# Query projection of 16 of 32 head groups by seven products of quarters, with the squares of the keys summed on ScalarE, in a gated two-layer decoder on one core

## The chip, the cores and the metric

The kernel runs on one core of a Trainium2 chip, written in Bass with the Tile framework, in float32 throughout. The metric is the device time of one execution in microseconds (us), the median of several executions. Inside a core five engines work side by side, each through its own list of instructions in order: TensorE (PE in the profile, with its weight loads as PEld) multiplies matrices into PSUM, VectorE (DVE), ScalarE (ACT) and GpSimd (POOL) work on elements, and SyncE (SP) issues transfers (DMA). ACT and POOL issue some transfers too, and then they are held in their own list until the issue is done.

## The reference, cut to what matters

x has 4 x 512 rows of 512 columns. A first layer (an attention over 256-column context rows and a linear layer of bit weights) is added to x with gates. Then comes the part that fills most of the time, cross attention with 16 heads of 128 columns, and last a layer of 16 experts for the first 512 rows, each row going to up to four of them:

```python
q = (layernorm(x) @ Wq).reshape(B, Sq, H, D)      # 512 -> 16 x 128
k = (ctx @ Wk).reshape(B, Skv, H, D)              # 256 -> 16 x 128
v = (ctx @ Wv).reshape(B, Skv, H, D)
q = q * rsqrt(mean(q*q, -1) + EPS) * gq           # rmsnorm of each head
k = k * rsqrt(mean(k*k, -1) + EPS) * gk
attn = softmax(einsum('bqhd,bkhd->bhqk', q, k) / sqrt(D))
x = x + tanh(g_xattn[1]) * (einsum('bhqk,bkhd->bqhd', attn, v).reshape(...) @ Wo)
x = x + tanh(g_ffn[1]) * experts(layernorm(x))    # only the first batch's rows are read and changed
```

## The kernel before

**Groups and steps.** The 16 heads are taken two at a time: a group m is one batch and one pair of heads, so there are 32 groups, eight for each of four batches, and 64 heads. After the first layer the program runs 64 steps, one for each head: step i is head h = i % 2 of group m = i // 2. A step has four quarters. Each quarter begins with `scores`, one matmul of 128 query rows against all 512 keys of this head, and then runs pieces of other work that a table assigns to it. An even step (h = 0) makes the keys and values of the next group (`keys_values`, quarters 0 and 1), the values product of an earlier head (`values(i - 2)`, quarter 2) and half of an output projection (`project`, quarter 3). An odd step (h = 1) makes the two heads' queries of the next group (`queries`, quarters 0 and 1), `values(i - 2)` in quarter 2 and the other half projection in quarter 3.

**The expert blocks.** From step 22 to step 55 each pair of steps also carries one expert block: rows turned (`rows_T`, even step, quarter 0), the two hidden products (`hidden`, quarters 1 and 2) with Tanh and product on ACT and DVE (`gate`, `gated`), then in the odd step the turned hidden rows (`hidden_T`, quarter 0) and `down` in quarter 2, whose result `keep_rows` stores. The rows are gathered back and added to x near the end (`add_row`).

**Order.** The order on every engine is the order in which the Python program emits instructions; nothing reorders it. `tick()` counts emitted matmuls, and `later(n, f)` emits f when n more have been counted. So work for DVE, ACT and POOL is put behind the matmul it belongs to by counts, and a list that waits holds up all that stands behind it.

**A score's way.** `scores` writes one of two PSUM banks (psS). On DVE the rows are scaled and their minimum taken in one instruction (L870, which empties the bank), ACT takes the exponential with its sum (L871), DVE takes the reciprocal (L877), scales (L878) and transposes in blocks of 32 into tP (L260). After a head's fourth such transpose SP issues 16 transfers of 64 KB (L268), which bring tP into the form that `values` reads (pT, tag big).

**Keys.** `keys_values` copies each PSUM bank into kn and v on ACT. Two ticks after its last matmul ACT squares all of kn in one instruction (L748); at four ticks DVE sums the squares (L752) and forms kss (L755), POOL raises to the power -1/2 (rk, L192) and multiplies kn by it (L759); at eleven ticks DVE transposes kn in blocks into tK (L770). ACT then issues one store to DRAM (k_d) and, at 18 ticks, four loads of kT.

**Queries.** `queries(m, h)` makes one head's queries, transposed, with 128x128 blocks of Wq as weights and 512 columns of the normalised, transposed rows (lx1, tag lnT) as the moving operand. ACT reads the bank twice, once for squares and once to scale into qT. The squares are then summed by DVE, PE and POOL into rq, which L870 uses for scaling.

```python
for k in range(KC):                                    # KC = 4
    nc.tensor.matmul(pp, wq[:, k, h * D : (h + 1) * D], lx1[b][:, k, :], ...)
```

The tag psA has three PSUM banks, which keys, queries, hidden, down and half of the projections take in turn; psO has one and psT two. wq, wkv and wo have two SBUF buffers each and are loaded by SP. In the profile a matmul of the code has two records.

Of the kernel before, what the change touches and what calls it, by code (L numbers as in the profile page):

```python
# [31 lines left out]
FCH = [(0, 128), (128, 128), (256, 96)]  # L32
NSLOT = 2 * NE - 1
SPILL = 1
TB = 32
# [19 lines left out]
def tile_gated_decoder(  # L55
# [51 lines left out]

    def col(n, tag):
        return tiny.tile([P, n], F32, tag=tag, name=tag)

# [95 lines left out]
    def rows_stats(b):  # L206

        stats = {}

        def chunk(c):  # L210
            if c == 0:
                stats["mv"] = tiny.tile([P, NC, 2], F32, tag="mv", name="mv")
            st = col(6, "st")
            nc.vector.bn_stats(st, x_sb[:, b * NC + c, :])
            nc.vector.bn_aggr(stats["mv"][:, c, :], st)
            if c == NC - 1:
                ve = col(NC, "ve")
                nc.vector.tensor_scalar(ve, stats["mv"][:, :, 1], EPS, None, ALU.add)
                stats["rs"] = col(NC, "rs")
                rsqrt(stats["rs"], ve, NC)  # L220

        return [lambda c=c: chunk(c) for c in range(NC)], stats

    def normalised(b, c, mv, rs):
        xn = row("xn", 2)
        nc.vector.tensor_scalar(
            xn, x_sb[:, b * NC + c, :], mv[:, c, 0:1], rs[:, c : c + 1], ALU.subtract, ALU.mult
        )
        return xn
# [96 lines left out]
    def l0_stats(b):  # L326

        pieces, stats = rows_stats(b)

        def gates():  # L330
            gate0[b] = gr = col(NC, "gr")
            nc.vector.tensor_scalar(gr, stats["rs"], tg[:, 0:1], None, ALU.mult)
            gm = col(NC, "gm")
            nc.vector.scalar_tensor_tensor(gm, stats["mv"][:, :, 0], -1.0, gr, ALU.mult, ALU.mult)
            for c in range(NC):
                x_c = x_sb[:, b * NC + c, :]
                later(c, lambda x_c=x_c, c=c: nc.scalar.activation(
                    x_c, x_c, AF.Identity, bias=gm[:, c : c + 1]
                ))

        return pieces[:-1] + [lambda: (pieces[-1](), later(3, gates))]
# [75 lines left out]
    def layer0_attention():  # L417
# [57 lines left out]

        load_wq(0)
        load_wq(1)
        load_wo(0)
# [15 lines left out]
        for h in range(G):  # L494
            queries(0, h)
        linear(NB - 1, turned0[NB - 1], [0, 1])

# [19 lines left out]
    def route():  # L517
# [20 lines left out]

        zero = row("xg", 1)
        nc.gpsimd.memset(zero, 0.0)  # L540
# [10 lines left out]
        ef_b = ef.unsqueeze(1).broadcast_to(CE)  # L551
        hit = small_tile([P, TOPK, NC, NE], "hit")
        for k in range(TOPK):
# [103 lines left out]
    def bias_row():  # L657
# [23 lines left out]
        yield  # L681
        brow.append(row("y", 2))
        nc.vector.tensor_copy(brow[0], pb)
# [17 lines left out]
    wq_of, wo_of = {}, {}  # L701
    q_of, sq_of, rq_of, kn_of, k_of, v_of, o_of = {}, {}, {}, {}, {}, {}, {}
    turned, moved, ends = {}, {}, {}
    n_heads = G * len(groups)

    def load_wq(m):
        t = work.tile([P, KC, GD], F32, tag="wq", name="wq")
        nc.sync.dma_start(t, wq_v[:, :, cols(m)])
        wq_of[m] = t

# [6 lines left out]
    def keys_values(m, chunks):  # L717
# [28 lines left out]
        def squares():  # L746
            st["sq"] = work.tile([P, NC, GD], F32, tag="sq", bufs=1, name="ksq")
            nc.scalar.activation(st["sq"], kn, AF.Square)  # L748

        def scale():  # L750
            kss = col(NC * G, "kss")
            nc.vector.tensor_reduce(  # L752
                kss, st["sq"].rearrange("p c (h d) -> p (c h) d", h=G), AX.X, ALU.add
            )
            nc.vector.tensor_scalar(kss, kss, 1.0 / D, EPS, ALU.mult, ALU.add)  # L755
            rk = col(NC * G, "rk")
            rsqrt(rk, kss, NC * G)
            kn_v = kn.rearrange("p c (h d) -> p c h d", h=G)
            nc.gpsimd.tensor_tensor(  # L759
                kn_v, kn_v,  # L760
                rk.rearrange("p (c h) -> p c h", h=G).unsqueeze(3).broadcast_to([P, NC, G, D]),
                ALU.mult,
            )
# [27 lines left out]
        later(2, squares)  # L791
        later(4, scale)
        later(11, turn)
# [3 lines left out]
    def queries(m, h):  # L797
# [21 lines left out]
        if h < G - 1:  # L819
            return  # L820
        n = G * S // TB
        st = {}

        def part():

            st["part"] = col(n, "part")
            nc.vector.tensor_reduce(
                st["part"], sq.rearrange("p h (j r) -> p (h j) r", r=TB), AX.X, ALU.add,
                apply_transpose=True,
            )  # L830
# [6 lines left out]
        def scale():  # L837

            own = col(n, "own")
            nc.vector.tensor_tensor(own, st["pq"][:, 0:n], mine, ALU.mult)  # L840
            v = col(G * NC, "qss")
            nc.vector.tensor_reduce(v, own.rearrange("p (c a) -> p c a", a=NT), AX.X, ALU.add)
            nc.vector.tensor_scalar(v, v, 1.0 / D, EPS, ALU.mult, ALU.add)  # L843
            rq_of[m] = col(G * NC, "rq")
            rsqrt(rq_of[m], v, G * NC)
# [319 lines left out]
    for c in range(NC):  # L1165
        for k in range(TOPK):
            put(last + 1 + c, k, lambda c=c, k=k: add_row(c, k))
    for b in range(1, NB):
        i = (b - 1) * NG * G + NG
        for j, f in enumerate(turned_rows(b, lx1, lnt)):  # L1170
            put(i + j // NC * (1 + j % NC), 3 if j >= NC else j, f)
        if b > 1:
            put(i, 3, lambda b=b: load_ctx(b))
# [13 lines left out]
    def step(i):  # L1187
        m, h = divmod(i, G)
        pieces = [[], [], [], []]
        if i >= G:  # L1190
            pieces[0 if i == n - 1 else 2].append(lambda: values(i - G))
        elif h > 0:
            pieces[3].append(lambda: tick(8))
        if i == n - 1:
# [7 lines left out]
        if h == 0:  # L1202
            if 0 < m < M - 1:
                pieces[0].append(lambda: keys_values(m + 1, [0, 1]))
                pieces[1].append(lambda: keys_values(m + 1, [2, 3]))
            if m + 2 < M:
                pieces[1].append(lambda: load_wq(m + 2))
                pieces[3].append(lambda: load_wkv(m + 2))
            if m >= 2:
                pieces[3].append(lambda: project(m - 2, [2, 3]))  # L1210
            if 2 <= m < M:
                pieces[3].append(lambda: later(4, lambda: load_wo(m)))
        elif i < n - 1:
            if m + 1 < M:
                pieces[0].append(lambda: queries(m + 1, 0))
                pieces[1].append(lambda: queries(m + 1, 1))
            if m >= 1:
                pieces[3].append(lambda: project(m - 1, [0, 1] if m < M else [0, 1, 2, 3]))
        for quarter in range(4):
            if i < n:  # L1220
                scores(i, quarter)
            for f in pieces[quarter] + extra.get((i, quarter), []):
                f()
# [73 lines left out]
```

## Time and profile before

| what | value |
|---|---|
| runs | 1455.59, 1457.45, 1457.69 us; median 1457.45 |
| profiled execution | 1457.03 us, span of the profile 1454.8 us |
| mean granted TensorE clock | 0.995 |
| busy in the span: PE, DVE, ACT, POOL | 1425.9, 936.0, 523.2, 285.5 us |
| matmuls of the queries (L807) | 512 records of 128x512, 231.3 us busy |
| matmuls of the scores (L856), keys and values (L733) | 512 records each, 262.5 and 231.8 us busy |
| squares of the keys (L748, ACT), their sums (L752, DVE) | 32 each, 1059 and 1216 ns in the mean |
| transfers of probabilities (L268) | 1008 of 64 KB, 2.0 us from issue to landing |

The lines of the profile name the line of the code, the engine, what is written and what is read, the shape and the count; behind the bar stand busy time, the mean length of one, and the engine's idle time before it with what ended it. The mean length of one matmul is longer than its share of the array, since matmuls run one behind the other in a pipeline: the interval between two starts is what a matmul costs.

### The profile page before, as it was taken

The page shows a single profiled execution, that of the slowest core. Times are in us where ns is not written, and L with a number is a line of the kernel's source. Part 1 is how long each engine was busy: PE and PEld are TensorE (multiplying, and loading weights), DVE is VectorE, ACT ScalarE, POOL GpSimd, SP SyncE. Part 2 cuts the span into 40 slices and gives each one's busy share as a digit, 9 for nine tenths or more (in the row PEclk, how much of TensorE's full clock was granted, in tenths as well). Part 3 has the DMA queues.
Part 4 walks back from the last instruction along what each step waited for, and adds up shares of the span by engine and source line. Part 5 has one row for each costly group of instructions (what it writes and reads, how often), then busy time and mean ns, then how long its engine had stood idle before and what let it go on. Part 6 is the DMA issues. An engine that isn't in the chain of part 4 may idle for free.

```text
span 1454.8 us, 13743 instructions
## 1 busy us (share of the span) xinstructions
PE 1425.9 (98%) x3745; PEld 669.9 (46%) x3745; DVE 936.0 (64%) x2160; ACT 523.2 (36%) x1196; POOL 285.5 (20%) x210
## 2 busy tenths in 40 slices
PE   7999998999999999999999999999999999999998
PEld 3544443444444444444444444444444444444444
DVE  4768857677776776665655565565565565557783
ACT  4642223333443334233333323333333323333331
POOL 1314414332111111111110111111011111002320
PEclk9999999999999999999999999999999999999999
DMA  7525016644544445555565565557566566635752
GB/s 254 174 73 189 1 44 162 158 131 132 136 133 136 134 134 171 170 173 177 174 173 175 174 215 168 170 165 200 158 185 191 144 200 192 177 113 162 200 145 77
DMA packets 155347, 226.90 MB, mean 156 GB/s; under 512 B 24576, under 2 KB 90640, under 8 KB 155264
## 3 DMA queue, kind: packets, MB, share of 16 engines
q1 hardware_dynamic: 127312, 177.86, 41.6%
q10 hardware_dynamic: 23040, 33.56, 7.4%
q0 software_dynamic: 4912, 14.53, 3.6%
q8 instruction: 33, 0.54, 0.2%
q14 instruction: 50, 0.41, 0.1%
HBM read 129.62 MB, written 30.17 MB: 110 GB/s over the span
## 4 chain that ended last, share of the span: by engine, by line
PE 81%; DVE 9%; ACT 3%; DMA 3%; SPq 3%; issue 1%; POOL 0%; ACTq 0%; POOLq 0%
PE psA L733 14%; PE psS L856 13%; PE psA L807 12%; PE psO L903 12%; PE psA L954 7%; PE psA L1029 6%; PE psO L954 4%; PE psT L954 3%; PE psA L1057 3%; PE psA L363 3%; SPq L268 3%; PE psA L691 1%; DMA big<-tP 1%; ACT prob L871 1%; DVE prob L870 1%; DVE tP L260 1%
## 5 line engine op out<-in xcount | busy, mean ns | idle before, releaser
L871 ACT ACTIVATE prob<-prob,top 128x512 f32<-128x512 f32 x256 | 184.8, 722 | 571.9 <-DVE prob L870 571.9
L856 PE MATMUL psS<-kT,qT 128*128 128x512 f32 x512 | 262.5, 596 | 1.0 <-DVE prob L870 1.0
L733 PE MATMUL psA<-wkv,ctx 128*128 128x512 f32 x512 | 231.8, 592 | 0.3 <-ACT v L728 0.3
L807 PE MATMUL psA<-lnT,wq 128*128 128x512 f32 x512 | 231.3, 592 | 0.0
L903 PE MATMUL psO<-big,v 128*128 128x512 f32 x504 | 226.6, 592 | 0.0
L870 DVE TENSOR_SCALAR_CACHE_REDUCE prob<-psS,rq 128x512 f32<-128x512 f32 x256 | 187.7, 734 | 53.2 <-PE psS L856 47.6
L260 DVE STREAM_TRANSPOSE tP<-prob 128x512 f32<-128x512 f32 x252 | 179.1, 711 | 9.0 <-DVE prob L878 1.1
L877 DVE RECIPROCAL rden<-den 128x1 f32<-128x1 f32 x256 | 40.7, 159 | 215.1 <-ACT prob L871 214.8
L807 PEld LDWEIGHTS psA<-lnT,wq 128*128 128x128 f32 x512 | 96.7, 190 | 118.6 <-issue 118.4
L903 PEld LDWEIGHTS psO<-big,v 128*128 128x128 f32 x504 | 95.7, 190 | 120.7 <-issue 116.2
L733 PEld LDWEIGHTS psA<-wkv,ctx 128*128 128x128 f32 x512 | 96.5, 190 | 118.8 <-issue 112.6
L192 POOL TENSOR_TENSOR rq<-qss,mhalf 128x8 f32<-128x8 f32 x32 | 53.2, 1661 | 493.0 <-DVE qss L843 493.0
L878 DVE TENSOR_SCALAR prob<-prob,rden 128x512 f32<-128x512 f32 x256 | 137.3, 536 | 9.0
L192 POOL TENSOR_TENSOR rk<-kss,mhalf 128x8 f32<-128x8 f32 x32 | 52.6, 1645 | 439.0 <-DVE rden L877 277.8
L856 PEld LDWEIGHTS psS<-kT,qT 128*128 128x128 f32 x512 | 92.9, 190 | 89.3 <-issue 68.9
L954 PE MATMUL psA<-wo,oT 128*128 128x512 f32 x256 | 123.3, 601 | 5.8 <-ACT oT L910 5.8
L1029 PE MATMUL psA<-gu,xgT 128*128 128x352 f32 x272 | 86.0, 459 | 0.0
L954 PEld LDWEIGHTS psA<-wo,oT 128*128 128x128 f32 x256 | 48.3, 191 | 68.3 <-issue 57.6
L770 DVE STREAM_TRANSPOSE tK<-kn 128x256 f32<-128x256 f32 x128 | 45.4, 412 | 39.1 <-POOL kn L759 39.1
L1029 PEld LDWEIGHTS psA<-gu,xgT 128*128 128x128 f32 x272 | 51.7, 190 | 37.9 <-issue 16.3
L954 PE MATMUL psO<-wo,oT 128*128 128x512 f32 x128 | 62.8, 613 | 0.0
L275 DVE SCALAR_TENSOR_TENSOR x_sb<-psA,tg,x_sb 128x512 f32<-128x512 f32 x80 | 57.8, 723 | 6.7 <-PE psA L691 3.8
(173 smaller groups left out, 1483.4 us busy)
## 6 DMA issues: line engine op xcount, KB each, us to landing
big<-tP SPq DMA_DIRECT2D x1008, 64.0 KB, 2.0
k_d<-tK ACTq DMA_DIRECT2D x32, 512.0 KB, 2.6
kT<-k_d ACTq DMA_DIRECT2D x128, 128.0 KB, 2.9
wq<-in_wq_dram SPq DMA_DIRECT2D x32, 512.0 KB, 3.7
wo<-in_wo_dram SPq DMA_DIRECT2D x32, 512.0 KB, 4.4
gu<-in_gate_dram SPq DMA_DIRECT2D x16, 704.0 KB
gu<-in_up_dram SPq DMA_DIRECT2D x16, 704.0 KB, 6.3
wkv<-in_wk_dram SPq DMA_DIRECT2D x32, 256.0 KB, 5.6
```

The costliest lines, as they stand in the source:

```text
L192: nc.gpsimd.tensor_tensor(out, v, mhalf[:, :n], ALU.pow)
L260: nc.vector.transpose(tP[:, :, c, :], e.rearrange("p (j r) -> p j r", r=TB))
L275: nc.vector.scalar_tensor_tensor(x_sb[:, t, :], src, gate, x_sb[:, t, :], ALU.mult, ALU.add)
L733: nc.tensor.matmul(pp, ctxs[b][:, k, c * P : (c + 1) * P], wkv[:, k, :, :].rearrange("p a n -> p (a n)"), start=(k == 0), stop=(k == CC - 1),)
L807: nc.tensor.matmul(pp, wq[:, k, h * D : (h + 1) * D], lx1[b][:, k, :], start=(k == 0), stop=(k == KC - 1))
L856: nc.tensor.matmul(sc, q_of[m][h][:, c * P : (c + 1) * P], k_of[m][:, :, h, :], start=True, stop=True)
L870: nc.vector.tensor_scalar(e, x, scale, 3.0e38, ALU.mult, ALU.min, accum_out=top)
L871: nc.scalar.activation(st["e"], st["e"], AF.Exp, bias=top, scale=-1.0, accum_out=st["den"])
L878: nc.vector.tensor_scalar(st["e"], st["e"], rden, None, ALU.mult)
L903: nc.tensor.matmul(po, v[:, k, h * D : (h + 1) * D], pT[:, :, k, :], start=(k == 0), stop=(k == NC - 1))
L954: nc.tensor.matmul(pp, oT[:, j, c * P : (c + 1) * P], wo[:, j, :], start=(j == 0), stop=(j == G - 1))
L1029: nc.tensor.matmul(st[a][:, :FF], st["xgT"][:, k * P : (k + 1) * P], st["gu"][:, a, k, :], start=(k == 0), stop=(k == KC - 1),)
```

## The change

The change has four parts.

1. **Seven products.** For the groups q with 12 <= q < 28 the queries of both heads are made together. Weights (two halves of the depth, two heads) and rows (two halves of the depth, two halves of the rows) are quarters of a 2x2 product, which seven products of quarters give instead of eight. The sums of weights are made by POOL (`combine`, four of 128x256 for each group), the sums of rows by DVE once for each batch (`combine_rows`, four of 128x512, for three batches). Each product is two matmuls of 256 columns. Four products are made in quarter 3 of the even step (`quarter_queries(q, 0)`), three in quarter 1 of the odd step (`quarter_queries(q, 1)`), in two banks (px, py) that are held in between; DVE (five additions of 128x256) and ACT (two copies) put the four results together. ACT then squares and scales both heads from SBUF.
2. **Order in these steps.** `values` in the odd step moves from quarter 2 to quarter 0; `project` of a group stands in quarters 2 and 3 of one odd step, behind `down`, instead of in an odd and the next even step; the loads of wo and wkv move with it.
3. **Keys' squares.** In all 32 groups ACT squares kn in eight instructions of 128x128, each with its sum (`accum_out`), two at a tick from the second to the fifth; DVE's sum is gone, and `scale` stands at six ticks instead of four.
4. **Buffers and places.** wq has one buffer instead of two, so its load waits for the last product with the old weights (group 1's is issued behind group 0's queries). Some tiles share tags (xn with y, a zero tile with xgT, brow with xg, hit with tK), and small columns have fewer buffers. The sixteen `add_row` stand three to a step over six steps instead of four to a step over four.

```diff
+SWITCH = (12, 28)
...
     def normalised(b, c, mv, rs):
-        xn = row("xn", 2)
+        xn = row("y", 2)
...
-        load_wq(0)
-        load_wq(1)
+        load_wq(0)()
...
         for h in range(G):
             queries(0, h)
+        load_wq(1)()
...
+    HS, HK = S // 2, KC // 2
+
     def load_wq(m):
-        t = work.tile([P, KC, GD], F32, tag="wq", name="wq")
-        nc.sync.dma_start(t, wq_v[:, :, cols(m)])
-        wq_of[m] = t
+        w = work.tile([P, KC, GD], F32, tag="wq", bufs=1, name="wq")
+        nc.sync.dma_start(w, wq_v[:, :, cols(m)])
+        if not by_quarters(m):
+            wq_of[m] = w
+            return lambda: None
+        sums = work.tile([P, 3, HK, D], F32, tag="wqs", bufs=1, name="wqs")
+        def quarter(h, a):
+            return w[:, a * HK : (a + 1) * HK, h * D : (h + 1) * D]
+        def combine():
+            s1, s2, s4 = (sums[:, j] for j in range(3))
+            s3 = quarter(1, 0)
+            nc.gpsimd.tensor_tensor(s1, quarter(1, 0), quarter(1, 1), ALU.add)
+            nc.gpsimd.tensor_tensor(s2, s1, quarter(0, 0), ALU.subtract)
+            nc.gpsimd.tensor_tensor(s3, quarter(0, 0), s3, ALU.subtract)
+            nc.gpsimd.tensor_tensor(s4, quarter(0, 1), s2, ALU.subtract)
+            wq_of[m] = [quarter(0, 0), quarter(0, 1), s4, quarter(1, 1), s1, s2, s3]
+        return combine
+
+    def combine_rows(b):
+        t = lx1[b]
+        sums = work.tile([P, 4, HK, HS], F32, tag="lxs", bufs=1, name="lxs")
+        def quarter(a, c):
+            return t[:, a * HK : (a + 1) * HK, c * HS : (c + 1) * HS]
+        t1, t2, t3, t4 = (sums[:, j] for j in range(4))
+        nc.vector.tensor_tensor(t3, quarter(1, 1), quarter(0, 1), ALU.subtract)
+        nc.vector.tensor_tensor(t1, quarter(0, 1), quarter(0, 0), ALU.subtract)
+        nc.vector.tensor_tensor(t2, quarter(1, 1), t1, ALU.subtract)
+        nc.vector.tensor_tensor(t4, quarter(1, 0), t2, ALU.subtract)
+        lxs_of[b] = [quarter(0, 0), quarter(1, 0), quarter(1, 1), t4, t1, t2, t3]
...
         def squares():
-            st["sq"] = work.tile([P, NC, GD], F32, tag="sq", bufs=1, name="ksq")
-            nc.scalar.activation(st["sq"], kn, AF.Square)
+            st["kss"] = col(NC * G, "kss", 3)
+            sq = work.tile([P, NC, GD], F32, tag="sq", bufs=1, name="ksq")
+            def chunk(c):
+                for h in range(G):
+                    at = slice(h * D, (h + 1) * D)
+                    nc.scalar.activation(
+                        sq[:, c, at], kn[:, c, at], AF.Square,
+                        accum_out=st["kss"][:, c * G + h : c * G + h + 1],
+                    )
+            for c in range(NC):
+                later(c, lambda c=c: chunk(c))
         def scale():
-            kss = col(NC * G, "kss")
-            nc.vector.tensor_reduce(
-                kss, st["sq"].rearrange("p c (h d) -> p (c h) d", h=G), AX.X, ALU.add
-            )
+            kss = st["kss"]
...
-        later(4, scale)
+        later(6, scale)
...
+    def quarter_queries(m, part):
+        ws, xs = wq_of[m], lxs_of[groups[m][0]]
+        def product(j, out, start):
+            for k in range(HK):
+                nc.tensor.matmul(
+                    out, ws[j][:, k, :], xs[j][:, k, :], start=start and k == 0, stop=k == HK - 1,
+                    skip_group_check=True,
+                )
+                tick(0.5)
+        if part == 0:
...
+            def second():
+                nc.scalar.copy(u2, px[:, 0:HS])
+                nc.vector.tensor_tensor(u2, px[:, HS:S], u2, ALU.add)
+            def fourth():
+                nc.vector.tensor_tensor(u3, py[:, 0:HS], u2, ALU.add)
+                nc.vector.tensor_tensor(q1[:, HS:S], py[:, HS:S], u3, ALU.add)
+            product(0, px[:, 0:HS], True)
+            product(5, px[:, HS:S], False)
+            later(0, second)
+            product(6, py[:, 0:HS], True)
+            product(4, py[:, HS:S], False)
+            later(0, fourth)
+            return
...
+        def upper():
+            nc.scalar.copy(q0[:, 0:HS], px[:, 0:HS])
+            nc.vector.tensor_tensor(q1[:, 0:HS], px[:, HS:S], u3, ALU.add)
+        def lower():
+            nc.vector.tensor_tensor(q0[:, HS:S], py[:, HS:S], u2, ALU.add)
+            for h in (1, 0):
+                nc.scalar.activation(sq[:, h, :], q_of[m][h], AF.Square)
+            for h in (0, 1):
+                nc.scalar.activation(q_of[m][h], q_of[m][h], AF.Identity, scale=gqk)
+        product(1, px[:, 0:HS], False)
+        product(3, px[:, HS:S], True)
+        later(0, upper)
+        product(2, py[:, HS:S], False)
+        later(0, lower)
+        square_sums(m, sq)
...
-            put(last + 1 + c, k, lambda c=c, k=k: add_row(c, k))
+            put(last + 1 + (c * TOPK + k) // 3, (c * TOPK + k) % 3, lambda c=c, k=k: add_row(c, k))
...
+        if (b + 1) * NG > SWITCH[0]:
+            put(2 * max(b * NG, SWITCH[0]) - 2, 1, lambda b=b: combine_rows(b))
...
+        q = m + 1
+        late, late_before = by_quarters(q), by_quarters(m)
         if i >= G:
-            pieces[0 if i == n - 1 else 2].append(lambda: values(i - G))
+            pieces[0 if i == n - 1 or h and late else 2].append(lambda: values(i - G))
...
+            if late and q < M:
+                pieces[3].append(lambda: quarter_queries(q, 0))
         elif i < n - 1:
-            if m + 1 < M:
-                pieces[0].append(lambda: queries(m + 1, 0))
-                pieces[1].append(lambda: queries(m + 1, 1))
+            if q < M and not late:
+                pieces[0].append(lambda: queries(q, 0))
+            if q < M:
+                pieces[1].append(lambda: (quarter_queries if late else queries)(q, 1))
+            if m + 2 < M:
+                pieces[2].append(lambda: later(6, load_wq(m + 2)))
+            if late:
+                pieces[2].append(lambda: project(m - 1, [0, 1]))
             if m >= 1:
-                pieces[3].append(lambda: project(m - 1, [0, 1] if m < M else [0, 1, 2, 3]))
+                pieces[3].append(lambda: project(m - 1, [2, 3] if late else [0, 1]))
+            if late and q < M:
+                pieces[3].append(lambda: later(2, lambda: load_wo(q)))
```

## The prediction

> **What bounds the kernel now.** I read the page's totals first, then busy time by stretch (its length, then busy PE, PEld, DVE, ACT and POOL with their instructions, clock, DMA share, GB/s), then PE's own waits.
>
> ```profile
> PE 1425.9 (98%) x3745; PEld 669.9 (46%) x3745; DVE 936.0 (64%) x2160; ACT 523.2 (36%) x1196; POOL 285.5 (20%) x210
> ...
> 440.00:480.00 40.00, 40.00 (x96) 17.77 (x95) 27.27 (x62) 16.22 (x37) 5.17 (x3) 1.00 0.50 143
> ...
> 880.00:920.00 40.00, 40.00 (x107) 19.07 (x106) 23.38 (x54) 13.28 (x31) 6.24 (x4) 1.00 0.59 179
> ...
> PE psA L954 <- ACT oT L910: 5.8, 5, 2.9
> ...
> PE psS L856 <- DVE prob L870: 1.0, 1, 1.0
> ```
>
> From 280 to 1360 us PE is busy in practically all of every 40 us, DVE in 22 to 31, ACT in 12 to 17. A busy PE can hide short gaps, so I counted: between 560 and 1240 us stand 1364 matmuls of 512 columns, 256 of 352, 141 of 128 and 32 of 32, and at the intervals found below they fill 679 of the 680 us. So TensorE is the bound, and its time saved in the expert stretch is time saved, as long as nothing else becomes late. The second line of waits shows how little is late today.
>
> **The cost of a narrow matmul.** The timeline of PE has unbroken rows of three widths (start, length, count). "us" runs from the first start to the last end, so the interval is (length less the mean duration of one) over (count less one).
>
> ```profile
> 894.06 3.60 PE L807 MATMUL psA<-lnT,wq 128*128 128x512 f32 x8
> ...
> 922.52 2.53 PE L1029 MATMUL psA<-gu,xgT 128*128 128x352 f32 x8
> ...
> 1443.93 1.05 PE L934 MATMUL psA<-big,v 128*128 128x128 f32 x8
> ```
>
> 512 columns: (3.60 - 0.592)/7 = 0.430 us. 352: (2.53 - 0.459)/7 = 0.296. 128: (1.05 - 0.275)/7 = 0.111. The line through the outer two gives 0.297 at 352, as measured, and 0.217 at 256. Each of these has a weight load of its own, recorded with 190 ns, and even at 111 ns between matmuls it does not show. A matmul of the code is two records (float32 goes in two passes: 32 groups of 8 in the code, 512 in the group's count). So the queries of one group cost 16 x 0.430 = 6.88 us; by quarters 7 products x 2 x 2 = 28 records x 0.217 = 6.08. Saved: 0.80 us a group, and for the 16 groups 12 to 27 **12.8 us**. The bounds are half of a wide one (0.215: 13.8 us) and the next wider row (0.296: a loss of 22.5 us); the line through both neighbours says the first is near.
>
> A rule speaks against this. The Trainium skill, "TensorE: Matmul & The Clock Gate", section "Back-to-back issue gap", gives about 81 ns a matmul at N=128 and 131 ns at N=512 for streams with weight loads: a narrow one would keep 62% of a wide one's price. By that, 256 columns would cost about 75% of 512, an estimate from that page, and the change would lose some 34 us. The rows here have 26%, in this kernel's own type, so they decide.
>
> **ScalarE's squares, in the expert steps.** One square of 128x1024 (1.07 us) and a DVE reduction (1.21) become eight of 128x128 with a sum each. The trace has no such form. Between: 0.25 us (a 128-column copy lets the next start 0.16 later, and reading a sum adds 0.09 behind L871) and 0.45 (266 ns for such a copy plus 188 for reading the sum, nothing overlapped). I take 0.33, nearer the overlap that every ACT row shows. ACT grows by 8 x 0.33 - 1.07 = 1.6 us a group and by about 0.9 in the quarter groups (two more copies and squares from SBUF), against 23 idle us in 40: no bound. What matters is who waits behind it. After the change four of the eight stand ahead of gate's Tanh (room: 923.25 to 925.09) and four behind the third softmax exponential.
>
> ```profile
> 923.25 1.07 ACT L748 ACTIVATE ksq<-kn 128x1024 f32<-128x1024 f32 x1
> ...
> 925.09 0.46 ACT L1038 ACTIVATE hh<-psA 128x352 f32<-128x352 f32 x1 [0.77 <-PE psA L1029]
> ...
> 926.81 0.72 ACT L871 ACTIVATE prob<-prob,top 128x512 f32<-128x512 f32 x1 [1.26 <-DVE prob L870]
> ...
> 897.55 2.40 ACTq L785 DMA_DIRECT2D kT<-k_d  x2
> 900.00 0.37 ACT L1050 COPY hT<-psT 128x256 f32<-128x256 f32 x1 [3.18 <-DMA kT<-k_d]
> ...
> 906.40 2.74 PE L1057 MATMUL psA<-dn,hT 128*128 128x512 f32 x6
> ```
>
> That exponential ends at 927.61, so the key factors kss come at 927.61 + 4 x 0.33 = 928.9 where L755 stood at 927.94: 1.0 us later (0.7 to 1.5). Behind kss on DVE wait the key transposes and the fourth softmax; behind that one's last step the sixteen DMAs of the probabilities; and behind some of those ACT waits, because the four loads of kT that it issues wait for them (the row of 2.40 us). The new add into u (about 0.40, from the 0.48 of L1043's 352 columns) also stands ahead of that transpose. So ACT comes free about 1.45 us later (1.1 to 1.9), and its next work is hT, which the block's last matmul, down, needs. Down itself moves forward: from the end of hidden_T (897.98) it was 8.42 us away; now there lie a score, the three last products (12 records) and a score: 0.86 + 12 x 0.217 + 0.86 less 0.16 of drain = 4.15. The copies begin 2.0 to 2.2 us after hidden_T in ten of the seventeen blocks and 2.5 to 3.1 (mean 2.83) in seven. Then 1.45 later, 0.47 to a copy done and seen: the ten just fit (4.0), the seven miss by 0.6. **Cost: 4 us**, 2 at the low end, 10 at the high. Nothing of this waits today.
>
> **The other edits of these steps.** DVE gets five additions of 128x256 a group (2.0 us) for the reduction of 1.21, and has 16 idle us of 40. Its stretch from down to the next step becomes dense: I place the next step's first softmax about 2.5 us later than now, and it catches up in the 3.2 us that DVE idles ahead of gate (922.36 to 925.58). Cost 0; if not, the fourth key matmul waits for its bank, under 1 us a group. Values moves ahead in odd steps, to the first quarter: its probabilities land about 12.6 us into the step before, 15 with that lag, and it lasts 22. Project goes behind down with all four chunks, so oT's copy gets 7 us instead of 0.9: a small gain. The weights' four sums on POOL, 128x256, are 0.6 to 0.8 us each by L688 (1306 ns at 512 columns): 3 us a group on an engine that is idle four fifths, queued behind rq, so no softmax waits for them; the load they wait for (3.7 us to land) is issued past the probabilities' DMAs on SP and has over 20 us until its first product. combine_rows, four additions of about 0.6, falls three times into DVE's idle time. The single wq buffer makes load_wq wait for the group's last product; SP has y_d's store and the next probabilities behind it, and both come later anyway. All 0.
>
> **The squares elsewhere.** The 16 plain groups have a lock in their path. In ten of them DVE's scaling of the fourth probabilities (0.49 us) meets POOL's product on kn and ends 0.28 us after it, whenever that ends:
>
> ```profile
> 376.76 1.90 POOL L759 TENSOR_TENSOR kn<-kn,rk 128x1024 f32<-128x1024 f32 x1
> ...
> 377.28 1.66 DVE L878 TENSOR_SCALAR prob<-prob,rden 128x512 f32<-128x512 f32 x1
> ```
>
> After the change both hang on kss: POOL's product starts 0.26 + 1.72 = 1.98 us after it, the scaling about 1.88. If the scaling goes first, the probabilities leave about 1.3 us earlier, ACT's wait ends earlier and part of the 5.8 us of PE's waits for oT goes, and with it the half clock behind the two long ones (0.91 and 0.92 in the 10 us behind 1360; some 1.7 us each). With squares at 0.45 the order is the same, 0.9 later. I take **-1.5 us**, from -6 (all waits gone) to +4 (a new wait of 0.3 in most).
>
> The Trainium skill, "SBUF — State Buffer", section "Who interferes with whom", has this as an exclusive lock and adds DVE operations with two SBUF inputs; it would make POOL's 3 us of new sums block DVE. The rows above agree on the lock; on two inputs no run here decides. If all of it fell on the path it would be 3 us a group, 48 in all, an estimate by that page; I count none, since DVE has idle time behind it.
>
> **The rest.** Tags shared in layer 0 and the later load of wq for group 1 (issued about 193 us, needed at 208.75) cost 0. Three output additions a step instead of four take DVE work of 0.72 us out of steps with PE waits (2.1 us at 1366) and put it beside the 1.0 at 1410: 0, within 2 either way.
>
> **Sum.** -12.8 + 4 - 1.5 = -10.3. The profiled execution took 1457.03 (span 1454.8 and 2.2 around it), so 1446.7; the median of the runs is 0.4 above it: **1447.0**.
>
> **The rivals.** (a) My forecast: faster, own range 1441.5 to 1454, chance 0.75. (b) ACT becomes the late engine: in every quarter group down waits for hT, or project for ACT's copies of the halves. Price: the shift beyond 1.6 us times 16; it decides from 0.8 us a group, where 12.8 is eaten; at 1.0 the time is 1457.5 + 3.2 = 1460.7. For it: the margin falls from 5.9 us to 0.15, and ACT waits for DMAs there in every block. Against: squares would have to take over 0.45 us. Chance 0.11, slower. (c) The plain groups lose what the others gain: squares at 0.45 and the lock unchanged make 0.9 us later, of which some 0.5 in 15 groups reaches PE, 7 us, with 4 in the others: 1456, no change to speak of; chance 0.10. (d) Narrow matmuls gain nothing: at 0.246 us for 256 columns 28 equal 16 wide ones; with the 4 us of waits 1461. Three rows on one line speak against it: slower, 0.04.
>
> Measurement tells 0.2%, about 3 us, from no change. Faster 0.78 (a, and 0.03 of c), same 0.07 (the rest of c), slower 0.15 (b and d). The range runs from (a)'s low end to part of (b), **1441.5 to 1458**.
>
> **What would show it.** PE: 448 records of 256 columns, 217 ns apart (eight in about 1.9 us); the counts of the old form halved; busy share unchanged. ACT: squares 0.33 apart. PE's waits: down on hT's copy, some 0.6 us in seven blocks, and fewer for oT. Scaling of the fourth probabilities at 0.49 us in the plain groups. I am wrong if down waits in all blocks, if PE shows idle time at the first or last product, or if a product's interval is over 0.23.

## The result, and the profile after

The changed kernel takes 1445.16 us in the median of six runs (before, in the same comparison: 1456.56); the ratio is 0.9917, with an interval of 0.9901 to 0.9934. One of the six, at a mean clock of 0.753, is left out of that ratio; the other five lie between 1441.6 and 1447.56, with a median of 1444.19. The forecast was 1447.0, range 1441.5 to 1458, faster. The profiled execution took 1444.19 (span 1442.5) against 1457.03 (1454.8): 12.8 us less, of which 12.3 in the span.

The totals of the page after. PE has 192 records more and 17 busy us less; ACT has gained 51.6 us, POOL 46.9, DVE 3.1.

```profile
PE 1408.8 (98%) x3937; PEld 703.2 (49%) x3937; DVE 939.1 (65%) x2220; ACT 574.8 (40%) x1708; POOL 332.4 (23%) x274
```

Busy time by stretch (length, then PE, PEld, DVE, ACT and POOL with their instructions, clock, DMA share, GB/s). As before, PE is busy throughout in plain and in expert stretches, so TensorE is still the bound.

```profile
440.00:480.00 40.00, 40.00 (x96) 17.89 (x95) 27.06 (x60) 17.01 (x58) 8.70 (x5) 1.00 0.44 131
880.00:920.00 40.00, 40.00 (x120) 21.70 (x119) 24.04 (x58) 16.30 (x51) 9.09 (x8) 1.00 0.60 181
```

The timeline of PE in an expert block of after: the first of the three last products and, behind the other two and a score, `down`.

```profile
769.09 1.03 PE L880 MATMUL psA<-lnT,wq 128*128 128x256 f32 x4
...
772.54 1.88 PE L1168 MATMUL psA<-dn,hT 128*128 128x512 f32 x4
```

Four narrow matmuls take 1.03 us and one alone 0.379 in the mean, so the interval is (1.03 - 0.379)/3 = 0.217 us, as the prediction has it; their weight loads (190 ns) do not show. hidden_T starts once in each block. In after (first fence) two such starts are 41.82 us apart, in before (second) 42.64:

```profile
851.53 0.49 PE L1159 MATMUL psT<-ident,hh 128*128 128x128 f32 x3
893.35 0.49 PE L1159 MATMUL psT<-ident,hh 128*128 128x128 f32 x3
```

```profile
854.85 0.49 PE L1048 MATMUL psT<-ident,hh 128*128 128x128 f32 x3
897.49 0.49 PE L1048 MATMUL psT<-ident,hh 128*128 128x128 f32 x3
```

That is 0.82 us a group where nothing waits, 13 us in sixteen groups. What waits is in PE's own waits of after (us in total, times, longest):

```profile
PE psT L245 <- DVE y L227: 4.6, 7, 1.1
...
PE psS L967 <- DVE x_sb L276: 2.8, 1, 2.8
...
PE psA L1065 <- issue: 2.0, 1, 2.0
PE psA L1168 <- ACT hT L1161: 1.9, 2, 0.9
PE psS L967 <- DMA kT<-k_d: 1.3, 1, 1.3
```

The wait for oT that led before (5.8 us, five times) is down to 1.1, and the 2.0 of the row with "issue", which is the same matmul at 248 us. Two waits are new in the expert steps: the transposes of the normalised rows (L245; four of the seven waits, 3.6 us between starts; the others are in layer 0), and `down` (L1168). I also summed the gaps between PE's starts beyond the intervals of their widths, and the summed gaps are what "gaps" means below. Between 560 and 1285 us they were 3.4 us before and are 9.2 after: 5.8 us are given back there. Elsewhere they fall by 4.0 us: 2.9 near 85 us, where before has half a clock for 6.8 us; 1.5 between 200 and 560 us; 4.0 between steps 56 and 60, where a wait of 2.1 us and the half clock behind it are gone; and a new wait of 2.84 us at 1397 takes 4.65 back with its own half clock. So PE's last matmul ends 11.2 us earlier (-12.8 + 5.8 - 4.0, to 0.2), and what follows it is 1.1 us shorter.

### The profile page after: what moved, and what is told of

It is laid out like the page before. It is cut to its first block, busy times and chain, and to the rows that moved or that the text cites. A ratio compares the mean times of both kernels' runs of the same rounds, so it can differ in the third digit from the quotient of the medians.

```text
span 1442.5 us, 14876 instructions
## 1 busy us (share of the span) xinstructions
PE 1408.8 (98%) x3937; PEld 703.2 (49%) x3937; DVE 939.1 (65%) x2220; ACT 574.8 (40%) x1708; POOL 332.4 (23%) x274
## 4 chain that ended last, share of the span: by engine, by line
PE 75%; DVE 12%; ACT 5%; DMA 3%; issue 2%; POOL 2%; SPq 1%; ACTq 0%; POOLq 0%
PE psA L775 13%; PE psS L967 12%; PE psO L1014 12%; PE psA L1065 6%; PE psA L857 6%; PE psA L880 5%; PE psA L1140 5%; PE psO L1065 3%; PE psT L1065 3%; PE psA L1168 2%; PE psA L364 2%; DVE x_sb L276 2%; ACT prob L982 2%; PE psA L694 1%; DVE prob L981 1%
## 5 line engine op out<-in xcount | busy, mean ns | idle before, releaser
L967 PE MATMUL psS<-kT,qT 128*128 128x512 f32 x512 | 262.4, 596 | 4.1 <-DVE x_sb L276 2.8
L775 PE MATMUL psA<-wkv,ctx 128*128 128x512 f32 x512 | 231.7, 592 | 0.3 <-ACT v L770 0.3
L981 DVE TENSOR_SCALAR_CACHE_REDUCE prob<-psS,rq 128x512 f32<-128x512 f32 x256 | 187.9, 736 | 27.9 <-PE psS L967 18.7
L775 PEld LDWEIGHTS psA<-wkv,ctx 128*128 128x128 f32 x512 | 96.5, 190 | 118.8 <-issue 108.6
L989 DVE TENSOR_SCALAR prob<-prob,rden 128x512 f32<-128x512 f32 x256 | 140.8, 550 | 9.0
L967 PEld LDWEIGHTS psS<-kT,qT 128*128 128x128 f32 x512 | 92.9, 190 | 78.7 <-issue 60.7
L857 PE MATMUL psA<-lnT,wq 128*128 128x512 f32 x256 | 115.6, 592 | 0.0
L857 PEld LDWEIGHTS psA<-lnT,wq 128*128 128x128 f32 x256 | 48.3, 190 | 59.3 <-issue 59.1
L795 ACT ACTIVATE ksq<-kn 128x128 f32<-128x128 f32 x256 | 75.3, 299 | 0.0
L276 DVE SCALAR_TENSOR_TENSOR x_sb<-psA,tg,x_sb 128x512 f32<-128x512 f32 x80 | 58.2, 727 | 6.7 <-PE psA L694 3.8
```

The source lines that it names most:

```text
L276: nc.vector.scalar_tensor_tensor(x_sb[:, t, :], src, gate, x_sb[:, t, :], ALU.mult, ALU.add)
L775: nc.tensor.matmul(pp, ctxs[b][:, k, c * P : (c + 1) * P], wkv[:, k, :, :].rearrange("p a n -> p (a n)"), start=(k == 0), stop=(k == CC - 1),)
L967: nc.tensor.matmul(sc, q_of[m][h][:, c * P : (c + 1) * P], k_of[m][:, :, h, :], start=True, stop=True)
L981: nc.vector.tensor_scalar(e, x, scale, 3.0e38, ALU.mult, ALU.min, accum_out=top)
L989: nc.vector.tensor_scalar(st["e"], st["e"], rden, None, ALU.mult)
```

## The experiments

My theory from the two traces: the products earn some 13 us, waits in the expert steps take 5.8 back, and the rest comes from the squares and from the clock. The main rival: the squares and the placing of steps gave the gain, and the products earned nothing after their waits.

**1. No quarters at all.**

```diff
-SWITCH = (12, 28)
+SWITCH = (32, 32)
```

> All 32 groups make their queries by eight wide products (SWITCH = (32, 32)); squares, tags, single wq buffer and the placing of the added rows stay as changed. Theory (the products earn 16 x 0.80 = 12.8 us and the new waits of the expert steps take 5.8 of them back: 2.2 for the turned hidden rows, 3.6 for the normalised rows): 1445.2 + 7.0 = 1452, within 2. Rival (the gain is the squares' and the placing's, and the seven products earn nothing after their waits): 1445. Second rival (the waits belong to the squares, not to the products, and stay): 1445.2 + 12.8 = 1458.

Measured: 1450.3 us, ratio 0.9961 (0.9948 to 0.9974). So the products are worth 6.1 us against after's median of 1444.19, and 6.4 by the ratios, where 7.0 were expected; the two intervals do not touch. The sum of gaps between 560 and 1285 us is 4.0 here: the waits of the expert steps came with the products, or with the order of these steps, which this edit takes back too. The profiled execution (span 1446.0) is one of this kernel's better ones: it has no half clock while PE works and only 2.1 us of gaps behind 1360 us, where after has 6.1.

**2. One square again, in the changed kernel.**

```diff
-                    nc.scalar.activation(sq[:, c, at], kn[:, c, at], AF.Square, accum_out=...)
+            nc.scalar.activation(st["sq"], kn, AF.Square)
...
+            nc.vector.tensor_reduce(kss, st["sq"].rearrange(...), AX.X, ALU.add)
-        later(6, scale)
+        later(4, scale)
```

> The changed kernel with the keys' squares as before: one square of 128x1024 on ScalarE, summed by VectorE, scaled at four ticks. Theory (steps 0 to 22, which hold plain groups alone, came out 2.2 us shorter, and in the quarter groups the sums cost the two waits for the turned hidden rows of 2.2): both vanish, 1445, within 2. Rival (VectorE's lag in the quarter groups is what counts, and the reduction of 1.21 us a group makes it worse): 1448 to 1452. Second rival (ScalarE's longer list is what costs, as the forecast had it): 1441.

Measured: 1447.84, ratio 0.9946 (0.9927 to 0.9965); the interval touches that of after. The waits say more: oT is late again, 7.3 us in four waits, 4.1 of them at 252 us.

```profile
PE psA L1057 <- ACT oT L1013: 7.3, 4, 4.1
```

So the sums on ScalarE shorten the way of the probabilities. `down` waits once, by 0.5 us, where after has 1.1 twice, so the wait for hT comes for the most part from the new squares, as the theory has it. The transposes of the normalised rows still wait (3.9 us with layer 0; in the expert steps 2.6, in two places, for 3.6 in four), so most of that wait does not come from the squares.

**3. The sums on ScalarE, alone, in the kernel before.** The edit is that of 2 the other way round.

> The kernel before with the eight squares and their sums on ScalarE alone, scaled at six ticks. Theory (in the plain groups the new form is worth about -0.2 us a group, as steps 0 to 22 show, and in the expert steps nothing waits): 1456.6 - 2 to -4 = 1453.5. Rival (c) of the prediction (later scaling reaches TensorE in the plain groups): 1458 to 1463. No effect: 1456.6.

Measured: 1450.71, ratio 0.9966 (0.9954 to 0.9978): 5.7 us less: more than the 2 to 4 of the theory, and the other way than rival (c). The wait for oT at 252 us falls from 3.08 us to 0.87, the one of 2.28 at 1368 is gone, and so are the two half clocks behind them (1.7 us each); a wait of 1.98 for transfers at 254 is new. In PE's waits oT is left with:

```profile
PE psA L962 <- ACT oT L918: 1.1, 2, 0.7
```

Runs 2 and 3 complete a square with before and after. By the ratios, the products with their order and the old squares (run 2) stand 7.9 us below before, the new squares alone (run 3) 5.0, and both together 12.1: the two gains nearly add up.

**4. Added rows by four, as before.**

```diff
-            put(last + 1 + (c * TOPK + k) // 3, (c * TOPK + k) % 3, lambda c=c, k=k: add_row(c, k))
+            put(last + 1 + c, k, lambda c=c, k=k: add_row(c, k))
```

> The changed kernel with the sixteen added rows four to a step over four steps, as before. Theory (the new wait of 2.84 us at 1397 and the half clock behind it, 4.65 us from step 60 to step 63, come from the added rows that now stand there; the 4.0 us gained in steps 56 to 60 come from their leaving): the two change places, 1445, within 2, with the wait back near step 58. Rival (the wait at 1397 belongs to the last queries' factors rq, not to the added rows, and the gain at step 56 has another cause): 1445 with the wait still at step 62. Second rival (only one of the two is moved): 1441 or 1449.

Measured: 1443.89, ratio 0.9913 (0.9892 to 0.9933), no difference that can be told. Waits of 1.6 and 1.7 us stand at 1392 and 1399, none at step 58. So the wait near 1397 does not need the added rows. Here the softmax that frees the score's bank starts 0.05 us behind the end of rq (1397.83 behind 1397.78); in after it starts 0.73 behind, with an added row of 0.74 ahead of it on DVE. The wait is rq's, as the rival has it, and at most 0.7 of it is the added row's. The gain at step 56 is not theirs either: it goes with the squares (3).

**5. `project` ahead of `down`.** This gives `down` 3.4 us more.

```diff
-            for f in more + pieces[quarter] if late and h and quarter == 2 else pieces[quarter] + more:
+            for f in pieces[quarter] + more:
```

> The changed kernel with project's first two chunks ahead of down in the odd quarter steps, so that down starts 3.4 us later after hidden_T. Theory (down is the only work that is short of time there, by 1.1 us in two blocks): both waits go, 2.2 us less, 1443, and in the other blocks nothing changes. Rival (b of the prediction: project too would wait, for the banks that ScalarE and VectorE still hold with the halves of the queries): new waits at project, 1446 to 1455.

Measured: 1458.66, ratio 1.0008 (0.9995 to 1.0022): the whole gain is gone. It looks like rival (b), but the timeline of POOL and DVE shows another cause:

```profile
788.42 0.72 POOL L730 TENSOR_TENSOR wqs<-wq 128x256 f32<-128x256 f32 x1 [22.40 <-DMA wq<-in_wq_dram]
...
791.28 1.67 POOL L193 TENSOR_TENSOR rq<-qss,mhalf 128x8 f32<-128x8 f32 x1
...
792.98 0.75 DVE L981 TENSOR_SCALAR_CACHE_REDUCE prob<-psS,rq 128x512 f32<-128x512 f32 x1 [2.87 <-POOL rq L193]
```

`later(6, load_wq(m + 2))` counts its six ticks from where it is emitted. With `down` first these end behind the factors rq; with `project` first they end three ticks earlier, and the four sums stand ahead of rq. There they wait 7 us for the load of wq (issued at 781.50), and the next head's first softmax waits for rq behind them. In after rq comes first:

```profile
781.14 1.68 POOL L193 TENSOR_TENSOR rq<-qss,mhalf 128x8 f32<-128x8 f32 x1 [19.48 <-DVE qss L954]
784.18 0.73 POOL L730 TENSOR_TENSOR wqs<-wq 128x256 f32<-128x256 f32 x1 [1.36 <-PE psS L967]
```

**6. The normalised rows' transposes two ticks later.**

```diff
-            later(3, turn)
-            later(4, lambda: nc.scalar.copy(
+            later(5, turn)
+            later(6, lambda: nc.scalar.copy(
```

> The changed kernel with the transposes of the normalised rows at five ticks instead of three, and their copies at six instead of four, in all steps. Theory (VectorE, which has five additions a group more, makes the normalised rows 0.3 to 1.3 us too late for TensorE in four expert steps, 3.4 us in all): two more ticks are 1.7 us, the four waits go, 1442. Rival (the lag of VectorE is the limit and shows up elsewhere, at the fourth key matmul or the next softmax): the time stays at 1445. Third (the later copies hold ScalarE in front of a softmax): over 1447.

Measured: 1438.19, ratio 0.9871 (0.9851 to 0.9891), clear of after's interval. The row of L245 is gone from PE's waits, and the gaps between 560 and 1285 us fall from 9.2 to 5.4, which leaves the two waits of `down` there. The profiled executions differ by 5.5 us. Of the other 1.7, some 1.5 lie in layer 0, where the same transposes waited too: four waits of 2.8 us in all are gone there, and one of 1.3 is new.

**7. 24 groups instead of 16.**

```diff
-SWITCH = (12, 28)
+SWITCH = (8, 32)
```

> Seven products for the 24 groups 8 to 31 instead of 12 to 27 (SWITCH = (8, 32)). Theory (a group saves 0.80 us wherever TensorE is the bound): eight groups more are 6.4 us less, 1439, if the plain steps have time for the sums. Rival (steps without an expert block are 17.5 us long against 21 and VectorE's and ScalarE's additions do not fit behind the matmuls): new waits of half a microsecond or more in each new group, 1444 to 1452.

Measured: 1461.86, ratio 1.0037 (1.0023 to 1.0051). The eight new groups lose more than the sixteen gained; PE waits 8.5 us in all for banks that `project` has not emptied (L775 behind L276). The sums stand ahead of rq here too, in the steps without an expert block.

**8. Keys scaled a tick later, in the plain groups.**

```diff
-        later(6, scale)
+        later(6 if by_quarters(m) else 7, scale)
```

> The changed kernel with the scaling of the keys at seven ticks instead of six in the plain groups alone, so that GpSimd's product on the keys starts 0.86 us later and VectorE's scaling of the fourth probabilities, which starts 0.15 to 0.19 us behind it in eight groups and then takes 2.0 us, comes first. Theory (the lock still holds the probabilities of these groups back by 1.5 us, and only at 248 to 253 us, where TensorE waits 3.6 us, does that reach the end): scaling at 0.49 us in all plain groups, 1443 to 1444. Rival (every plain group pays for the lock): 1435. Second rival (the later keys are what TensorE then waits for at 253): 1446 to 1448.

Measured: 1442.18, ratio 0.9902 (0.9885 to 0.9920), within after's interval. The mechanism is there: scaling of the fourth probabilities takes 0.49 us in all the plain groups that the lock held, DVE is busy 12 us less (927.0), and the kT wait at 253 is gone: the gaps between 200 and 280 us fall from 6.2 to 4.1. In the other plain groups the lock cost DVE time and PE nothing.

**9. `project` ahead of `down`, with the sums behind rq.** As 5, and:

```diff
-                pieces[2].append(lambda: later(6, load_wq(m + 2)))
+                pieces[2].append(lambda: later(10, load_wq(m + 2)))
```

> As the run with project ahead of down, and the four sums of weights emitted ten ticks after the load of wq instead of six, so that they stand behind the queries' factors rq in GpSimd's list as they do in the changed kernel. Theory (the 13.5 us lost there come from the sums, which came to stand ahead of rq and wait 7 us for the load; the swap itself costs nothing and gives down 3.4 us): 1443 to 1445, no wait for the turned hidden rows. Rival (rival b of the prediction: the copies and additions of the halves make project wait): 1450 to 1459, with PE's waits at project in most expert steps.

Measured: 1444.2, ratio 0.9911 (0.9896 to 0.9926): the 13.5 us of run 5 are back, so they were POOL's order. No wait for hT is left, yet nothing is won: in the same two blocks (645 and 985 us) `project` now waits 1.1 and 1.4 us. That is rival (b) in part: `project` waits in two blocks, though for oT's copy and not for the copies of the halves.

**10. 24 groups, with the sums behind rq.** The edits of 7 and of 9's second diff together.

> Seven products for the 24 groups 8 to 31, and the four sums of weights at ten ticks instead of six. Theory (what the 24 groups lost was GpSimd's list: in steps without an expert block the sums stood ahead of rq and waited for the load of wq, so the next head's scores waited 3 to 5 us; behind rq they wait for nobody): 1439 to 1441. Rival (VectorE's five additions and ScalarE's copies do not fit behind the shorter plain steps): 1445 or more, with waits of TensorE in the eight new groups.

Measured: 1462.33, ratio 1.0041 (1.0025 to 1.0056). My theory for run 7 falls: the sums follow rq now, and the time stays. The gaps behind 1285 us sum up to 22 us, against 7 in after. DVE's list is full there:

```profile
1334.57 0.71 DVE L276 SCALAR_TENSOR_TENSOR x_sb<-psT,tg,x_sb 128x512 f32<-128x512 f32 x1
1335.19 1.87 DVE L276 SCALAR_TENSOR_TENSOR x_sb<-y,tw,x_sb 128x512 f32<-128x512 f32 x2
...
1336.98 0.74 DVE L276 SCALAR_TENSOR_TENSOR x_sb<-psA,tg,x_sb 128x512 f32<-128x512 f32 x1
...
1337.78 1.61 PE L775 MATMUL psA<-wkv,ctx 128*128 128x512 f32 x3 [3.23 <-DVE x_sb L276]
```

From 1329.24 to 1338.4 DVE works with one gap of 0.9 us: four chunks of `project`, the added rows and the softmax meet in a stretch in which PE has no expert block to do. The bank that the keys need is emptied by the last addition, which starts at 1336.98. That explains this wait, and one of 3.0 us at 1376 has the same releaser; half a clock follows each. The longest wait of the last four groups, 5.15 us at 1415, is a score's (L967 behind the softmax, L981) and was not taken apart. The first four (8 to 11) cost 4.5 us in four waits between 541 and 580 against the 3.2 they save, and were not taken apart further.

**11. Runs 6 and 8 together.**

> The two edits that gained something alone, together: the normalised rows' transposes two ticks later, and the keys' scaling one tick later in the plain groups. Theory (different waits in different steps, so the gains of 7.0 and 3.0 us add up): 1435. Rival (both gained by the same half-clock stretch near the end or the same wait at 248 us): 1438.

Measured: 1437.26, ratio 0.9864 (0.9848 to 0.9879), the best ratio, clearly under after's; whether it beats run 6 alone can't be told.

**12. And the loads of kT behind the copies of hT.**

```diff
-        later(18, take_in)
+        later(21 if by_quarters(m) else 18, take_in)
```

> The two edits together, and the four loads of kT three ticks later in the quarter groups, so that ScalarE issues them behind the copies of the turned hidden rows and of oT instead of ahead of them. Theory (what still makes down wait in two blocks, 2.7 us by the profile of the two edits, is ScalarE held in those issues; nothing before the next step needs kT): copies of the turned hidden rows about 1 us after hidden_T instead of 2.7 to 3.6, no wait at down, 1437.3 - 2.7 = 1434.5. Rival (the issues hold ScalarE just as long behind the copies, and the copies of the queries' halves then come late): 1437 or more, with waits of TensorE at the next product or at the first score of the next step.

Measured: 1438.45, ratio 0.9887 (0.9870 to 0.9905), no gain over 11. hT's copies come 0.04 us behind hidden_T in most blocks instead of 2.6, and nothing waits at `down`. But in the same two blocks as in 9, `project` waits now (1.6 and 1.5 us, and under 0.45 in three more), for DVE's additions to the queries:

```profile
641.26 0.42 DVE L914 TENSOR_TENSOR qT<-psA,u 128x256 f32<-128x256 f32 x1
...
641.73 1.99 PE L1065 MATMUL psA<-wo,oT 128*128 128x512 f32 x4 [1.44 <-DVE qT L914]
```

So it does not help to make hT alone earlier in these two blocks: in runs 9 and 12 whatever comes first in its place waits about as long.

## Why the prediction was right, point by point

**The narrow matmul: right to the digit.** The line through the outer widths gave 0.217 us, measured 0.217; 0.80 us a group, measured 0.82 where nothing waits. What the Trainium skill ("TensorE: Matmul & The Clock Gate", section "Back-to-back issue gap") gives for narrow streams does not hold for these float32 rows. Rival (d) is out.

**`down` and hT: the right wait, from a wrong shift.** The term was 4 us, in seven blocks by 0.6. Measured: 2.2 us, in two blocks by 1.09. A square with its sum costs 0.29 us, not 0.33:

```profile
881.02 0.29 ACT L795 ACTIVATE ksq<-kn 128x128 f32<-128x128 f32 x1
...
881.31 0.29 ACT L795 ACTIVATE ksq<-kn 128x128 f32<-128x128 f32 x1
```

And the copies begin 2.95 us behind hidden_T in the mean of thirteen blocks where they began 2.40: a shift of 0.55, not 1.45. In two more it is 4.82, from 2.47 and 2.87; in the first and the last of the seventeen it falls from 2.0 to 0.04. In the two with 4.82 DVE has a chunk of row statistics in the same step; the score's exponential comes late, and the probabilities leave late. ACT is then held in its second pair of kT loads:

```profile
637.84 0.72 ACT L982 ACTIVATE prob<-prob,top 128x512 f32<-128x512 f32 x1 [3.89 <-DVE prob L981]
...
639.26 3.78 ACTq L835 DMA_DIRECT2D kT<-k_d  x2
643.08 0.37 ACT L1161 COPY hT<-psT 128x256 f32<-128x256 f32 x1 [4.42 <-DMA kT<-k_d]
```

**VectorE's lag "cost 0": the step that failed.** I placed the next step's first softmax 2.5 us later and let it catch up ahead of gate; if not, the fourth key matmul was to wait. What waited was none of these. In four steps the rows of the next batch are normalised at that very point, and their transposes on PE come three ticks behind, 2.58 us after the step's first score. In before the rows' instruction starts 0.57 us after that score in all four steps, and in run 1, without quarters, again 0.57; in after it is 2.28 to 2.84. Whether the five additions make this lag, or the chunks of `project` that now all stand in the odd step, no run takes apart. In two of the four, at 657 and 1040 us, POOL's new sums add 0.4 us to it: the same instruction (L227, in before L226) takes 0.98 and 0.93 us beside them and 0.53 in before. The prediction had counted this lock at nothing. Before (first fence) and after:

```profile
656.48 0.53 DVE L226 TENSOR_SCALAR xn<-x_sb,mv,rs 128x512 f32<-128x512 f32 x1
```

```profile
656.95 0.72 POOL L730 TENSOR_TENSOR wqs<-wq 128x256 f32<-128x256 f32 x1 [2.39 <-PE psA L775]
656.98 0.98 DVE L227 TENSOR_SCALAR y<-x_sb,mv,rs 128x512 f32<-128x512 f32 x1
...
658.01 0.66 PE L245 MATMUL psT<-ident,y 128*128 128x128 f32 x4 [1.14 <-DVE y L227]
```

This is 3.6 us that the sum did not have (run 6 gives them back). With hT's 2.2 the waits are 5.8 where I had 4. I had followed DVE's lag through the softmax alone, and not to the pieces that stand in only some of the steps.

**The plain groups: a term too small, for a reason that was half wrong.** I had -1.5 (from -6 to +4); run 3 gives -5.7. The lock was to go, since scaling starts 1.88 us behind kss and POOL's product 1.98. The product does, but scaling starts 2.16 behind it: the order is the other one by 0.19 us, and in eight of the middle groups the lock holds scaling for 2.0 us. (The prediction counts ten groups with the lock in before; the trace has thirteen, with scaling between 0.72 and 1.68 us, each ending 0.28 behind the product.)

```profile
406.26 0.17 DVE L805 TENSOR_SCALAR kss<-kss 128x8 f32<-128x8 f32 x1 [0.91 <-ACT ksq L795]
...
408.23 1.90 POOL L809 TENSOR_TENSOR kn<-kn,rk 128x1024 f32<-128x1024 f32 x1
408.42 1.99 DVE L989 TENSOR_SCALAR prob<-prob,rden 128x512 f32<-128x512 f32 x1
```

In two of the late groups POOL has a gather to issue ahead of rk, the product starts 0.78 us behind scaling, and this takes 0.49; there the wait of 2.1 us at 1366 is gone, with its half clock. A margin of 0.10 us between two estimates was no ground for an order.

**The rivals.** (b) shows in two blocks: 2.2 us at `down` in after, 2.5 at `project` in run 9 and, with three small waits, 4 in run 12. The one place where a chain like it cost 13 us was POOL's list (run 5), which I had called free because rq stands ahead of the sums: true, by three ticks. (c) is refuted by run 3. **The rest**: DVE's added rows within 2 us, as run 4 has it; layer 0 differs by a half clock alone.

**The sum**, then: products -12.8 by the forecast; waits +5.8 for +4; the squares, the clock and the end together some -5 for -1.5. The total of -12.3 was forecast as -10.3, and two misses of opposite sign lie in it, so that the closeness is in part luck.

## What to carry to other kernels

A stream's price per instruction is read from unbroken rows of several widths; a line through them beat a general rule here. When an in-order engine gets more work, follow its lag to the pieces that stand in only a few steps, and not just to the work of every step. Work emitted by a count of ticks changes its place in a third engine's list when something ahead of it is reordered: look at who then stands behind whom, above all behind a load.

## What the runs showed of the hardware

**Half clocks make part of the spread.** The granted clock falls to 0.5 for 3.41 us or a multiple of it, behind some waits of PE and not behind others: none behind the 2.0 us at 248 in after, one behind the 2.84 at 1397. The same wait of 3.0 us near 82 us, which every kernel here has, is followed by 6.83 us of half clock in before, 3.41 in run 2 and none in after. Eight value matmuls then take 5.26 us instead of 3.60:

```profile
1397.32 1.20 PE L967 MATMUL psS<-kT,qT 128*128 128x512 f32 x2 [2.84 <-DVE x_sb L276]
...
1398.32 5.26 PE L1014 MATMUL psO<-big,v 128*128 128x512 f32 x8
```

Run 12's kernel took 1434.46 us at a mean clock of 1.000 and 1441.69 at 0.995: half a per cent, 7.2 us. Taking (1 - clock) of its time off each run leaves medians of 1450 to 1451.5 for before, 1446.5 for runs 1 and 3, 1441.6 for after and 1432 for run 11. This is a rough estimate, from clocks with three digits: it narrows the spread of run 9's kernel from 4.4 to 0.7 us, but leaves that of after at 5.9. What a removed wait is worth also depends on whether it would have brought a half clock. The Trainium skill, "TensorE: Matmul & The Clock Gate", section "HAM oscillation — how this bites in real kernels", warns of idle gaps over about 3.4 us; here 2.28 us (before, at 1368) and 2.84 were enough.

**Additions with two inputs from SBUF wait for GpSimd too.** Beside its product on kn, the addition of an expert's row (L276, two inputs from SBUF) takes 1.43 us instead of 0.74, in two groups; the same line with its first input from PSUM stays at 0.71. The Trainium skill, "SBUF — State Buffer", section "Who interferes with whom", says so of operations with two SBUF inputs; the prediction had left that undecided.

```profile
1338.76 1.90 POOL L809 TENSOR_TENSOR kn<-kn,rk 128x1024 f32<-128x1024 f32 x1
1339.14 0.71 DVE L276 SCALAR_TENSOR_TENSOR x_sb<-psT,tg,x_sb 128x512 f32<-128x512 f32 x1
1339.77 1.43 DVE L276 SCALAR_TENSOR_TENSOR x_sb<-y,tw,x_sb 128x512 f32<-128x512 f32 x1
```
